# Moving the bias products behind the first x products in the head of a recurrent kernel

## The chip, the cores and the metric

The kernel runs on one core of a Trainium2 chip. The metric is the device time of one execution in microseconds (us), as the median of several runs.

## What is computed

The input x has 16 sequences of 256 steps with 512 features. A GRU cell runs over the steps, and its states feed an expert-choice layer; x is added at the end. What matters here is the cell, in float32:

```
gi = x @ W_ih + b_ih            # 512 -> 3 * 512
gh = h @ W_hh + b_hh
r = sigmoid(i_r + h_r);  z = sigmoid(i_z + h_z)
n = tanh(i_n + r * h_n)
h = (1 - z) * n + z * h         # 256 steps, one after the other
```

The first state is `cond_2048`. The biases are not zero. For r and z both biases can be summed; for n, `b_hh` stands inside the product with r, so it is kept apart. After the recurrence come router logits, a softmax, the choice of the 256 strongest tokens of each of 16 experts, one matrix product with the expert's weights, and a weighted sum.

## The kernel before

**Tiling.** A step has 16 rows. Two steps form a pair, and the products x @ W_ih are made for a pair at once. The 512 output features are split into four groups of 128 partitions in a bank: `quadrant(j)` names 32 partitions of a bank, and four products with `tile_position=(0, 32 * j)` fill the four quadrants side by side. Six PSUM banks hold the sums: `ra` (r gate and input part of n, 256 columns), `hn` (hidden part of n) and `zz` (z gate), each twice, for even and odd pairs. All products add to what the bank holds (`start=False`), so each bank is first given a value.

**The head.** What runs before step 0 is written out by hand, with a fixed order on every engine:

- `begin_sums` (L108) fills a bank with products of zeros. `keep_clock(n)` (L470) repeats this n times on a bank called `idle`, which is otherwise unused; it only keeps TensorE working. It is called with 22 and, behind the x products, with 2.
- `load_rows` (L228) loads W_ih, then W_hh, half on SyncE's queue and half on ScalarE's, in the gate order r, n, z.
- GpSimd's queue loads the biases in three transfers (L288), then x of the first two pairs in eight (L273, `load_pairs(0, 2, ...)`), then clears `c0` and loads the initial state into it in four (L292). A transfer of this queue uses one of eight semaphores in turn, so the ninth waits until the first has landed.
- `biases(i)` (L305) multiplies a column of ones with the bias rows, into the banks of both pairs. VectorE copies the sums of one of them to `bias` and `nb` in SBUF (L481 to L483). They are needed by all later pairs, whose banks ScalarE presets from them (L421 to L433).
- `turn_x` (L255) transposes x of one pair on VectorE; `x_part` (L435, products at L445) adds x @ W_ih of that pair.
- VectorE turns the initial state and copies it to `hs` (L491, L492).

**The steps.** `h_part` (L449, products at L458) adds h @ W_hh in the order r, n, r, n, z. ScalarE makes r (L516), VectorE forms the argument of tanh, ScalarE makes tanh and z, and VectorE the new state, in two halves (L565 to L590). The next step's products need that state. From step 2 on the x products of later pairs, and from the second group of eight steps on the expert's products, fill TensorE's time while it would wait.

Of the kernel before, what the change touches and what calls it, by code (L numbers as in the profile page):

```python
# [13 lines left out]
ALU = mybir.AluOpType  # L14
# [4 lines left out]
def kernel(  # L19
# [34 lines left out]
    nc = tc.nc  # L54
    B, T, D = x.shape
    E = router_w.shape[1]
    P = 128
# [50 lines left out]
    def begin_sums(bank):  # L108

        n = bank.shape[-1]  # L110
        for j in range(KC):
            nc.tensor.matmul(
                bank[QD * j : QD * (j + 1)],
                zero,
                zero[:, 0:E].unsqueeze(1).to_broadcast([P, n // E, E]),
                start=True,
                stop=True,
                tile_position=(0, QD * j),
            )
# [69 lines left out]
    with (  # L189
# [14 lines left out]
        bias = wts.tile([P, 3, P], F32, name="bias")  # L204
        nb = wts.tile([P, P], F32, name="nb")
        rb = wts.tile([P, E], F32, name="rb")

        b_raw = xs[0:2, NG - 4 : NG - 1, :]
        b_n = xs[0:1, NG - 1, :]
# [7 lines left out]
        ra = [bank[:, 0 : 2 * P].rearrange("p (g d) -> p g d", d=P) for bank in banks[0:2]]  # L217
        hn = [bank[:, 0 : 2 * P] for bank in banks[2:4]]
        zz = [bank[:, 0:P] for bank in banks[4:6]]

        def quadrant(j, m=QD):
            return slice(QD * j, QD * j + m)

        def columns(ap, j):

            return ap.rearrange("p (c j i) -> p j c i", j=KC, i=QD)[:, j]

        def load_rows(dst, src, form):  # L228

            rows = src.rearrange(form, c=KC)  # L230
            for h in range(2):
                ks = slice(KC // 2 * h, KC // 2 * (h + 1))
                queues[h].dma_start(out=dst[:, ks, :], in_=rows[:, ks, :])
# [3 lines left out]
        def load_xa(g, xa, j, qs):  # L237

            for o in range(2):
                q = QD * j + B * o  # L240
                qs[o].dma_start(
                    out=xa[q : q + B],
                    in_=x[:, g * TG + o : (g + 1) * TG : 2, j * P : (j + 1) * P],
                )
# [10 lines left out]
        def turn_x(g, xa, pairs=slice(0, TG // 2)):  # L255
            if g not in xT:
                xT[g] = xtp.tile([P, TG // 2, P], F32, name="xt")
            nc.vector.transpose(  # L258
                xT[g][:, pairs, :].rearrange("p q (c r) -> p q c r", c=KC),
                xa[:, pairs, :].rearrange("p q (i c) -> p q c i", c=KC),  # L260
            )
# [5 lines left out]
        with tc.manual_schedule(engines={ET.SP, ET.Activation, ET.Pool}):  # L267
            def load_pairs(p, n, queue):

                for j in range(KC):  # L270
                    for i in range(n):
                        at = 2 * (p + i)
                        queue.dma_start(  # L273
                            out=xa0[quadrant(j), p + i, :],
                            in_=x[:, at : at + 2, j * P : (j + 1) * P].rearrange("b o d -> o b d"),
                        )

            for i, gate in enumerate((0, 2, 1)):
                load_rows(wih[:, :, i, :], w_ih[:, gate * D : (gate + 1) * D], "(p c) n -> p c n")
            for gate in (0, 2, 1):  # L280
                load_rows(whh[:, :, gate, :], w_hh[:, gate * D : (gate + 1) * D], "(c p) n -> p c n")

            for dst, src in (
                (b_raw[0:1], b_ih.rearrange("(o g d) -> o g d", o=1, d=D)),
                (b_raw[1:2], b_hh.rearrange("(o g d) -> o g d", o=1, d=D)),
                (b_n, b_hh[2 * D :].rearrange("(o d) -> o d", o=1)),
            ):
                nc.gpsimd.dma_start(out=dst, in_=src)  # L288
            load_pairs(0, 2, nc.gpsimd)
            nc.gpsimd.memset(c0, 0.0)  # L290
            for j in range(KC):
                nc.gpsimd.dma_start(  # L292
                    out=c0[QD * j : QD * j + B, :].rearrange("b (c i) -> b c i", c=KC), in_=columns(cond, j)
                )
            load_pairs(2, TG // 2 - 2, nc.sync)
            for j in range(KC):
                load_xa(1, xa1, j, (nc.sync, nc.sync))
            nc.sync.dma_start(out=ewr[:, :, E:], in_=expert_w.rearrange("(c p) n -> p c n", c=KC))
            nc.sync.dma_start(out=ewr[:, :, 0:E], in_=router_w.rearrange("(c p) n -> p c n", c=KC))
            nc.sync.dma_start(out=rb, in_=router_b.rearrange("(o e) -> o e", o=1).to_broadcast([P, E]))  # L300
            nc.sync.dma_start(out=eb, in_=expert_b.rearrange("(o d) -> o d", o=1).to_broadcast([P, D]))

        def biases(i):  # L305
            for dst, rows in (
                (ra[i][:, 0, :], b_raw[:, 0, :]),
                (ra[i][:, 1, :], b_raw[0:1, 2, :]),
                (hn[i][:, 0:P], b_n),
                (zz[i], b_raw[:, 1, :]),  # L310
            ):
                for j in range(KC):
                    nc.tensor.matmul(
                        dst[quadrant(j)],
                        ones[0 : rows.shape[0]],
                        columns(rows, j),
                        start=False,
                        stop=True,
                        tile_position=(0, QD * j),
                        skip_group_check=True,  # L320
                    )
# [3 lines left out]
        def of_step(ap, odd):  # L325
            return ap.rearrange("p (c q b) -> p c q b", q=2, b=B)[:, :, odd, :]
# [108 lines left out]
        def x_part(p, k, z):  # L435
            g, pair = divmod(p, TG // 2)
            lhs = xT[g][:, pair, QD * k : QD * (k + 1)]
            for j in range(KC):
                q = quadrant(j)
                dst, rhs = (  # L440
                    (zz[p % 2][q], columns(wih[:, k, 2, :], j))
                    if z
                    else (ra[p % 2][q], columns(wih[:, k, 0:2, :].rearrange("p g d -> p (g d)"), j))
                )
                nc.tensor.matmul(  # L445
                    dst, lhs, rhs, start=False, stop=(k == KC - 1), tile_position=(0, QD * j), skip_group_check=True
                )
# [20 lines left out]
        idle = ps_m.tile([P, D], F32, name="idle", tag="pe")  # L468

        def keep_clock(n):  # L470

            for _ in range(n):
                begin_sums(idle)

        with tc.manual_schedule(engines={ET.PE, ET.DVE}):
            for bank in banks:
                begin_sums(bank)
            keep_clock(22)
            biases(1)
            biases(0)  # L480
            nc.vector.tensor_copy(bias[:, 0:2, :], ra[1])  # L481
            nc.vector.tensor_copy(nb, hn[1][:, 0:P])
            nc.vector.tensor_copy(bias[:, 2, :], zz[1])  # L483
            for pair in range(2):
                turn_x(0, xa0, slice(pair, pair + 1))
            for z in (False, True):
                for pair in range(2):
                    for k in range(KC):
                        x_part(pair, k, z)
            keep_clock(2)  # L490
            nc.vector.transpose(turned, c0)  # L491
            nc.vector.tensor_copy(hs[:, :, 0, :], of_step(turned, 0))  # L492
        make_masks()
# [6 lines left out]
        with tc.manual_schedule(engines={ET.PE, ET.Activation, ET.DVE, ET.Pool, ET.SP}):  # L500
# [4 lines left out]
            for s in range(T):  # L505
                p, odd = divmod(s, 2)
                g, c = divmod(s, TG)
# [105 lines left out]
                elif g + 2 < NG:  # L613
                    if c == KC:
                        xa_next = new_xa()
                    j = c - KC
# [271 lines left out]
```

## Time and profile before

| | |
|---|---|
| median of 3 runs | 1164.77 us (1163.73 to 1165.15) |
| the profiled execution | 1164.63 us, its span 1162.8 us |
| VectorE busy | 703.6 us (61%) |
| ScalarE busy | 336.1 us (29%) |
| GpSimd busy | 100.0 us (9%) |
| granted TensorE clock, mean | 0.996 |

The span reaches from the first to the last instruction of the profiled execution; the rest of its time lies around it. The page divides the span into 40 slices of about 29 us, so the whole head lies in the first. "PEclk" is the clock that TensorE was granted, as a share of the full one. In a timeline each row has the start, the busy time, the engine, the line and the operation, with like instructions merged.

### The profile page before, as it was taken

Reading aid. Unit: us, or ns where it says so; the run is one execution under the profiler, and the core shown is the slowest. Engines: PE = TensorE matmul, PEld = TensorE weight load, DVE = VectorE, ACT = ScalarE, POOL = GpSimd, SP = SyncE. Lnnn points to the kernel's source line nnn. Section 1 sums busy time; section 2 is a strip of 40 time slices with the busy share of each in tenths; the row PEclk is TensorE's granted clock in tenths of the full one; section 3 lists DMA queues with packets and bytes.
Section 4 is the critical chain, followed back from the end, with each engine's and each line's share of the span. In section 5 each row is a group of like instructions: output and inputs, shape, how many; then the busy total and the mean of one; then the engine's idle time right before and its main releaser. Section 6 shows DMA issues by size and latency. Waiting matters only on the chain. (4 is left out here: it accounts for less than half of the span.)

```text
span 1162.8 us, 79365 instructions
## 1 busy us (share of the span) xinstructions
PE 1147.7 (99%) x36025; PEld 1018.4 (88%) x36025; DVE 703.6 (61%) x4078; ACT 336.1 (29%) x1444; POOL 100.0 (9%) x412
## 2 busy tenths in 40 slices
PE   7999999999999999999999999999999999999998
PEld 4899999999999999999999999999999999989742
DVE  1656665666666666666665666666656666665675
ACT  0323223232323232323232322332223222243320
POOL 3000010000000000000000000000000000000000
PEclk8999999999999999999999999999999999999999
DMA  7200000000000000000000000000000000000017
GB/s 231 76 23 20 21 18 22 21 19 19 20 21 20 21 20 21 20 21 21 20 20 21 21 20 18 22 21 20 18 23 20 21 18 23 20 16 14 3 54 240
DMA packets 48854, 38.01 MB, mean 33 GB/s; under 512 B 7968, under 2 KB 40800, under 8 KB 48512
## 3 DMA queue, kind: packets, MB, share of 16 engines
q1 hardware_dynamic: 46272, 29.56, 8.7%
q8 instruction: 283, 4.64, 1.6%
q10 hardware_dynamic: 1632, 3.15, 0.8%
q14 instruction: 59, 0.48, 0.1%
q0 software_dynamic: 608, 0.19, 0.1%
HBM read 24.47 MB, written 8.39 MB: 28 GB/s over the span
## 5 line engine op out<-in xcount | busy, mean ns | idle before, releaser
L458 PE MATMUL gates<-whh,hs 128*16 128x128 f32 x24576 | 723.2, 273 | 3.4 <-DVE hs L590 3.3
L458 PEld LDWEIGHTS gates<-whh,hs 128*16 128x16 f32 x24576 | 675.6, 103 | 9.5 <-DVE hs L590 4.1
L445 PE MATMUL gates<-wih,xt 128*32 128x256 f32 (+1 forms) x8192 | 385.7, 327 | 4.0 <-DVE xt L258 4.0
L445 PEld LDWEIGHTS gates<-wih,xt 128*32 128x32 f32 x8192 | 256.0, 110 | 65.9 <-DVE xt L258 4.3
L516 ACT ACTIVATE r<-gates 128x128 f32<-128x128 f32 x256 | 71.1, 278 | 614.1 <-PE gates L458 614.1
L520 DVE COPY seen<-r 1x1 f32<-1x1 f32 x256 | 36.3, 142 | 330.2 <-ACT r L516 330.2
L569 ACT ACTIVATE t<-t 128x64 f32<-128x64 f32 x512 | 102.9, 248 | 131.6 <-DVE t L567 131.6
L576 DVE STREAM_TRANSPOSE nT<-t 128x64 f32<-128x64 f32 x512 | 100.3, 234 | 49.0 <-ACT t L569 49.0
L579 DVE STREAM_TRANSPOSE zT<-zs 128x64 f32<-128x64 f32 x512 | 121.6, 237 | 0.2 <-issue 0.2
L590 DVE TENSOR_TENSOR hs<-v,nT 128x32 f32<-128x32 f32 x512 | 101.6, 198 | 21.7
L587 DVE TENSOR_TENSOR v<-u,zT 128x32 f32<-128x32 f32 x512 | 104.5, 204 | 8.8
L407 PE MATMUL pe<-ewr,ht 128*32 128x128 f32 x1920 | 97.0, 273 | 0.0
L565 DVE TENSOR_TENSOR t<-r,gates 128x64 f32<-128x64 f32 x512 | 89.7, 217 | 0.0
L567 DVE TENSOR_TENSOR t<-t,gates 128x64 f32<-128x64 f32 x512 | 88.4, 214 | 0.0
L407 PEld LDWEIGHTS pe<-ewr,ht 128*32 128x32 f32 x1920 | 63.6, 110 | 17.4
L582 DVE TENSOR_TENSOR u<-hs,nT 128x32 f32<-128x32 f32 x512 | 78.3, 153 | 0.0
L570 ACT ACTIVATE zs<-gates 128x128 f32<-128x128 f32 x256 | 71.0, 277 | 0.0
L137 PE MATMUL pe<-ewr,ht 128*32 128x256 f32 (+1 forms) x848 | 64.5, 442 | 0.5 <-ACT pe L160 0.5
L617 POOL COPY xa<-hs 32x1 f32<-32x1 f32 x120 | 21.4, 179 | 478.2 <-DVE hs L590 297.4
L333 POOL COPY ht<-hs 128x128 f32<-128x128 f32 (+1 forms) x128 | 46.8, 396 | 160.9 <-DVE hs L590 153.1
L249 POOL COPY xs<-hs 1x1 f32<-1x1 f32 x128 | 22.7, 178 | 338.5 <-DVE hs L590 333.5
L137 PEld LDWEIGHTS pe<-ewr,ht 128*32 128x32 f32 x848 | 25.9, 109 | 27.0 <-issue 16.8
(102 smaller groups left out, 310.1 us busy)
## 6 DMA issues: line engine op xcount, KB each, us to landing
xs<-in_x_dram SPq DMA_DIRECT2D x128, 64.0 KB
xa<-in_x_dram SPq DMA_DIRECT2D x248, 32.0 KB
out_dram<-xs SPq DMA_DIRECT2D x31, 256.0 KB
wih<-in_L_cond_W_ih_dram SPq DMA_DIRECT2D x3, 512.0 KB
wih<-in_L_cond_W_ih_dram ACTq DMA_DIRECT2D x3, 512.0 KB
whh<-in_L_cond_W_hh_dram SPq DMA_DIRECT2D x3, 512.0 KB
whh<-in_L_cond_W_hh_dram ACTq DMA_DIRECT2D x3, 512.0 KB
ewr<-in_L_ffn_expert_w_dram SPq DMA_DIRECT2D x1, 1024.0 KB
```

The lines of the kernel that those rows point to most:

```text
L137: nc.tensor.matmul(pe[q, cols], ht[:, g, k, q], ewr[:, k, E:][:, cols], start=False, stop=(k == KC - 1), tile_position=(0, QD * j), skip_g ...
L407: nc.tensor.matmul(pes[g][quadrant(j), at : at + P], ht[:, g, k, quadrant(j)], ewr[:, k, E + P * quarter : E + P * (quarter + 1)], start=( ...
L445: nc.tensor.matmul(dst, lhs, rhs, start=False, stop=(k == KC - 1), tile_position=(0, QD * j), skip_group_check=True)
L458: nc.tensor.matmul(dst[quadrant(j, m)], lhs, columns(whh[:, k, gate_, :], j), start=False, stop=(k == KC - 1), tile_position=(0, QD * j), ...
L565: nc.vector.tensor_tensor(t[half], r[:, cols], hn[p % 2][:, cols], ALU.mult)
L567: nc.vector.tensor_tensor(t[half], t[half], ra[p % 2][:, 1, cols], ALU.add)
L569: nc.scalar.activation(t[half], t[half], AF.Tanh)
L576: nc.vector.transpose(nT[half], t[half])
L579: nc.vector.transpose(zT[half], zs[:, halves[half][1]])
L582: nc.vector.tensor_tensor(u[half], hs[:, halves[half][2], slot(s), :], of_step(nT[half], odd), ALU.subtract)
L587: nc.vector.tensor_tensor(v[half], u[half], of_step(zT[half], odd), ALU.mult)
L590: nc.vector.tensor_tensor(hs[:, halves[half][2], slot(s + 1), :], v[half], of_step(nT[half], odd), ALU.add)
```

## The change

In GpSimd's queue the eight transfers of x stand first and the three of the biases behind them. The bias products no longer go into the banks of the sums. They are made once, behind the x products and the two rounds of `keep_clock`, into the four 128-column parts of the `idle` bank, which at that point holds zeros. VectorE copies them to `bias` and `nb` and adds them to the sums that the two pairs' banks already hold; ScalarE writes `nb` into the two `hn` banks. Then follow, on VectorE, the turn and the copy of the initial state. 16 bias products take the place of 32. The number of `keep_clock` rounds stays.

```
+            load_pairs(0, 2, nc.gpsimd)
             for dst, src in (
                 (b_raw[0:1], b_ih.rearrange("(o g d) -> o g d", o=1, d=D)),
                 (b_raw[1:2], b_hh.rearrange("(o g d) -> o g d", o=1, d=D)),
                 (b_n, b_hh[2 * D :].rearrange("(o d) -> o d", o=1)),
             ):
                 nc.gpsimd.dma_start(out=dst, in_=src)
-            load_pairs(0, 2, nc.gpsimd)
             nc.gpsimd.memset(c0, 0.0)
...
-        def biases(i):
-            for dst, rows in (
-                (ra[i][:, 0, :], b_raw[:, 0, :]),
-                (ra[i][:, 1, :], b_raw[0:1, 2, :]),
-                (hn[i][:, 0:P], b_n),
-                (zz[i], b_raw[:, 1, :]),
-            ):
+        def biases(bank):
+
+            for i, rows in enumerate((b_raw[:, 0, :], b_raw[0:1, 2, :], b_raw[:, 1, :], b_n)):
                 for j in range(KC):
                     nc.tensor.matmul(
-                        dst[quadrant(j)],
+                        bank[quadrant(j), P * i : P * (i + 1)],
                         ones[0 : rows.shape[0]],
                         columns(rows, j),
...
             keep_clock(22)
-            biases(1)
-            biases(0)
-            nc.vector.tensor_copy(bias[:, 0:2, :], ra[1])
-            nc.vector.tensor_copy(nb, hn[1][:, 0:P])
-            nc.vector.tensor_copy(bias[:, 2, :], zz[1])
             for pair in range(2):
                 turn_x(0, xa0, slice(pair, pair + 1))
             for z in (False, True):
                 for pair in range(2):
                     for k in range(KC):
                         x_part(pair, k, z)
             keep_clock(2)
+            biases(idle)
+
+            nc.vector.tensor_copy(bias, idle[:, 0 : 3 * P].rearrange("p (g d) -> p g d", d=P))
+            nc.vector.tensor_copy(nb, idle[:, 3 * P :])
+            for pair in range(2):
+                nc.scalar.copy(hn[pair][:, 0:P], nb)
+                nc.vector.tensor_tensor(ra[pair], ra[pair], bias[:, 0:2, :], ALU.add)
+                nc.vector.tensor_tensor(zz[pair], zz[pair], bias[:, 2, :], ALU.add)
             nc.vector.transpose(turned, c0)
             nc.vector.tensor_copy(hs[:, :, 0, :], of_step(turned, 0))
```

## The prediction

> **What bounds the kernel now.** I read the page's engine rows, its slices and its costliest group first, then the timeline of the first 27 us engine by engine, then the windows, because the change touches only what runs before the first of 256 recurrence steps.
>
> ```profile
> PE 1147.7 (99%) x36025; PEld 1018.4 (88%) x36025; DVE 703.6 (61%) x4078; ACT 336.1 (29%) x1444; POOL 100.0 (9%) x412
> ...
> PEclk8999999999999999999999999999999999999999
> ...
> L458 PE MATMUL gates<-whh,hs 128*16 128x128 f32 x24576 | 723.2, 273 | 3.4 <-DVE hs L590 3.3
> ```
>
> TensorE is busy all the way and its clock is full everywhere but in the first slice. The recurrence is one serial chain, so a head that hands over 1 us earlier is worth 1 us, and nothing behind it absorbs that. The question is when the first L458 product starts, and at which clock. The timeline of GpSimd, TensorE and VectorE in the head (start, busy time, engine, line; idle time before and what ended it in brackets):
>
> ```profile
> 1.33 0.64 POOL L288 DMA_DIRECT2D xs<-in_L_cond_b_ih_dram  x1 [0.47 <-issue]
> 1.97 0.97 POOL L288 DMA_DIRECT2D xs<-in_L_cond_b_hh_dram  x2
> 2.93 3.02 POOL L273 DMA_DIRECT2D xa<-in_x_dram  x5
> 7.06 0.59 POOL L273 DMA_DIRECT2D xa<-in_x_dram  x1 [1.12 <-DMA xs<-in_L_cond_b_ih_dram]
> 8.65 1.18 POOL L273 DMA_DIRECT2D xa<-in_x_dram  x2 [1.00 <-DMA xs<-in_L_cond_b_hh_dram]
> ```
>
> ```profile
> 3.45 6.51 PE L112 MATMUL idle<-zero 128*32 128x512 bf16 x88
> 9.89 1.96 PE L313 MATMUL gates<-xs,ones 2*32 2x128 f32 x64
> 15.88 7.56 PE L445 MATMUL gates<-wih,xt 128*32 128x256 f32 x128 [4.03 <-DVE xt L258]
> 23.26 0.61 PE L112 MATMUL idle<-zero 128*32 128x512 bf16 x8
> 23.70 2.79 PE L458 MATMUL gates<-whh,hs 128*16 128x128 f32 x96
> ```
>
> ```profile
> 10.60 0.42 DVE L481 COPY bias<-gates 128x256 f32<-128x256 f32 x1 [9.71 <-PE gates L313]
> 10.94 0.28 DVE L482 COPY nb<-gates 128x128 f32<-128x128 f32 x1
> 11.14 0.28 DVE L483 COPY bias<-gates 128x128 f32<-128x128 f32 x1
> 15.42 0.40 DVE L258 STREAM_TRANSPOSE xt<-xa 128x128 f32<-128x128 f32 x1 [4.00 <-DMA xs<-in_cond_dram]
> 16.39 0.41 DVE L258 STREAM_TRANSPOSE xt<-xa 128x128 f32<-128x128 f32 x1 [0.57 <-DMA xa<-in_x_dram]
> ```
>
> GpSimd issues three bias transfers, then x; its last three x transfers wait until the bias transfers have landed. TensorE ends the biases at 11.85 and sits idle for 4.03 us until x is there (the releaser named at 15.42 is the initial state's transfer; by order it is x of pair 0, which shares its semaphore). The windows show the clock (length, PE busy, PEld, DVE, ACT, POOL, then PEclk, DMA share, GB/s):
>
> ```profile
> 6.64:10.06 3.42, 3.42 (x72) 1.52 (x64) 0.00 (x0) 0.00 (x0) 2.00 (x5) 1.00 1.07 327
> 10.06:13.47 3.41, 1.79 (x64) 1.52 (x56) 0.82 (x3) 1.28 (x1) 3.17 (x10) 1.00 1.06 334
> 13.47:16.88 3.41, 1.00 (x12) 0.54 (x16) 0.81 (x2) 0.00 (x0) 0.02 (x1) 0.50 1.06 338
> 16.88:20.30 3.42, 3.42 (x40) 1.55 (x36) 1.46 (x9) 0.00 (x0) 0.30 (x1) 0.50 1.05 386
> 20.30:23.71 3.41, 3.41 (x103) 2.61 (x99) 0.00 (x0) 0.00 (x0) 0.00 (x0) 1.00 0.26 84
> ```
>
> The clock was halved from 13.47 to 20.30, one stretch of 6.83 us, after 1.6 us of idle time in a window that was 52% busy. The halved clock cost the x products half of the 4.42 us from 15.88 to 20.30.
>
> **x earlier.** The eight x transfers now start at 1.33 and follow at 3.02/5 = 0.60 us each, so the seventh (the last of pair 0) starts at 4.96 and the eighth at 5.56. From issue to landing the transfers of this queue took 5.4 us (first bias) to 6.7 us (median of x); the last one of before was issued at 9.24 and turned at 16.39, 7.15 us. I take 7.15, as the DMA engines are as full here (share 1.07), and 5.4 as the other end. Pair 0 is then there at 12.1 (10.4 at the early end) and its products start 0.48 us later as in the rows above (15.40 to 15.88): 12.6 instead of 15.88. The first two gates of wih land by 9.7 in the trace and its third by 14.4, both in time.
>
> **The x products.** Their 7.38 us (15.88 to 23.26) are 4.42 halved and 2.96 full, so 5.17 us at full clock. From 12.6 that gives an end at 17.8 at full clock throughout, 19.5 if the clock is halved from 13.47 to 16.88, and 21.2 if it is halved to 20.30. The window 10.06 to 13.47 would now be busy for 0.9 us instead of 1.79, so a drop is as likely as before; since TensorE now works from 12.6 on, I take the recovery one window earlier than in the trace: 19.5.
>
> **Biases behind it.** The two warming rounds take 0.44 (23.26 to 23.70), and the bias products are half as many, 1.96/2 = 0.98. Their three transfers now wait for the first x transfers to land (about 8 to 9 us) and take 6.5, so they land near 16, under the x products; without that cover every us late is a us lost. The four transfers of the initial state wait for later x transfers as they do now, and stay near 10.3 to 12. Products end at 19.5 + 0.44 + 0.98 = 20.9.
>
> **The new stretch on VectorE.** Before, bias copies and the turning of the initial state lay under other work. Now they stand between the bias products and step 0: a 384-column copy, a 128-column copy, two 256-column sums, two 128-column sums, the turn and the copy of the state. The starts 10.60, 10.94 and 11.14 in the trace give 0.34 us for 256 columns of a copy and 0.20 for 128. So 0.47 + 0.20 + 2 x (0.34 + 0.20) = 1.75 us. The trace has no sum of that size; the sums of the recurrence that read a bank (L565, two of 64 columns in 0.35 us, 0.22 each) start 0.13 apart, which lies on the line of the copies, so I take the copies' price. The upper end is their full duration in place of their spacing, 0.42 and 0.28, 0.3 us more; less than the copies is 0.1 at most. The state's turn and copy took 0.55 us from start to end, and handing over from and to TensorE some 0.27. Together 2.57. Behind these instructions on VectorE wait the state's copy and the small mask operations; the latter have 1.6 us until the first sigmoid ends. Step 0 then starts at 23.5 in place of 23.70: the 3.2 us won in front have gone.
>
> **ScalarE.** In the built order the copies of the n bias into two banks come before the first sigmoid, and there are two table loads where there was one at 10.10, each behind VectorE. A load took 1.28 us. The n bias is there 0.75 us into the stretch, the load ends at 2.05, the copy (0.27) at 2.3, the n products need it at 3.0. The second load ends near 3.8, the first sigmoid is due at 2.57 + 1.56 = 4.1 (23.70 to 25.26 in the trace). I cost both at nothing; uncovered they cost 1.28 each. [...]
>
> **The clock in the recurrence.** TensorE now idles 2.57 us between bias products and step 0, behind 0.98 us of products on two rows only. In the phase of the profile, 20.30 to 23.71 would be busy for about 0.85 us (25%), less than the 52% after which the clock was halved. Then 23.71 to 30.54 (6.83 us, as in the trace) runs at half clock: step 0 has 2.79 - 0.21 = 2.58 us of products left, which take 5.16, and step 1 loses 0.2, together 2.8. The other ends are 1.7 (one window of 3.41, half of it lost) and nothing. I take 2.8, from the only stretch that the trace has. [...]
>
> **Sum** against the profiled execution (1164.63, span 1162.8, 1.8 us around it; the median 1164.77 is 0.14 above): -0.2 + 2.8 = +2.6, so 1167.2. A measurement of this kernel can tell about 0.2% (2.3 us) from no change, so the bounds are 1162.4 and 1167.1.
>
> **Rivals.** Forecast, slower (0.37): clock halved in the x products for one window, and again as the recurrence begins, 1167.2. Slower still (0.10): halved to 20.30, head +1.5, and again, 1164.6 + 1.5 + 2.8 = 1168.9; or x lands no earlier because the DMA engines are full until 16.9, head + 0.98 + 2.57, 1168.2. No measurable change (0.36): only one of the two falls happens; x products at full clock and a fall at step 0, -1.9 + 2.8, 1165.5; a fall in the x products alone, 1164.4 to 1166.1. Faster (0.17): neither gap halves the clock, head 23.70 to 21.8, 1162.7, and with x at the early end 1.7 us less, 1161.0. It decides where a gap of 2.6 us lies across two windows, so that each stays busier than the 52%. For it speaks that both gaps are shorter than the 4.03 of before; against it, that they are two, and that the bias products no longer fill the first one. That the change does not do what it says is the landing case above.
>
> **How the numbers follow.** The faster case lies mostly between 1161.0 and 1163, the slowest at 1168.9, with 0.5 for the sums: 1162.2 to 1169.4 leaves out about 2 in 10. Faster by over 0.2% 0.17, within 0.36, slower 0.47 (0.37 and 0.10).
>
> **What would show it.** First x products near 12.6; VectorE busy for some 2.3 us with TensorE idle before step 0; step 0 at about 23.5; a halved clock beginning within 1 us of it and step 0 lasting about 6.5 us instead of 4.0. A first L458 product before 22 with a full clock behind it would refute the forecast, as would a first sigmoid that waits for a table load.

## The result, and the profile after

The changed kernel takes 1168.7 us (median of 8 runs, 1167.02 to 1171.08); the kernel before took 1164.7 us beside it. The ratio is 1.0038 (95% interval 1.0029 to 1.0047): slower by some 4 us. The forecast was 1167.2 us, within 1162.2 to 1169.4. The profiled execution took 1168.76 us, its span is 1167.0 us, 4.2 us over that of before.

The page still shows TensorE busy nearly throughout, with 99% turned into 98%; the clock's row is the same, since slices of 29 us are too coarse for what follows.

```profile
PE 1147.4 (98%) x35993; PEld 1009.6 (87%) x35993; DVE 704.2 (60%) x4081; ACT 337.8 (29%) x1447; POOL 99.7 (9%) x412
...
PEclk8999999999999999999999999999999999999999
```

The timeline of GpSimd and then of TensorE, as shown of before:

```profile
1.44 4.88 POOL L273 DMA_DIRECT2D xa<-in_x_dram  x8 [0.58 <-issue]
8.43 0.51 POOL L289 DMA_DIRECT2D xs<-in_L_cond_b_ih_dram  x1 [2.10 <-DMA xa<-in_x_dram]
9.15 1.12 POOL L289 DMA_DIRECT2D xs<-in_L_cond_b_hh_dram  x2 [0.21 <-issue]
```

```profile
3.45 5.58 PE L112 MATMUL idle<-zero 128*32 128x512 bf16 x88
13.79 7.64 PE L439 MATMUL gates<-wih,xt 128*32 128x256 f32 x128 [4.76 <-DVE xt L258]
21.25 0.61 PE L112 MATMUL idle<-zero 128*32 128x512 bf16 x8
21.79 1.08 PE L307 MATMUL idle<-xs,ones 2*32 2x128 f32 x32
25.25 4.42 PE L452 MATMUL gates<-whh,hs 128*16 128x128 f32 x96 [2.38 <-DVE hs L489]
30.91 2.83 PE L452 MATMUL gates<-whh,hs 128*32 128x128 f32 x96 [1.24 <-DVE hs L587]
```

The x transfers are issued without a break (4.88 us for eight) and the bias transfers wait for them (2.10 us before the first). The x products start 2.1 us earlier than before (13.79, 15.88), but step 0 starts 1.55 us later (25.25, 23.70), as 2.38 us of idle time stand in front of it, and its products then take 4.42 us in place of 2.79. What VectorE and ScalarE do in the new gap:

```profile
22.94 0.56 DVE L482 COPY bias<-idle 128x384 f32<-128x384 f32 x1 [8.19 <-PE idle L307]
23.41 0.28 DVE L483 COPY nb<-idle 128x128 f32<-128x128 f32 x1
23.61 0.42 DVE L486 TENSOR_TENSOR gates<-gates,bias 128x256 f32<-128x256 f32 x1
23.94 0.29 DVE L487 TENSOR_TENSOR gates<-gates,bias 128x128 f32<-128x128 f32 x1
...
25.00 0.20 DVE L489 COPY hs<-nT 128x64 f32<-128x64 f32 x1
```

```profile
23.78 1.28 ACT L485 ACT_TABLE_LOAD   x1 [23.78 <-DVE nb L483]
25.07 0.47 ACT L485 COPY gates<-nb 128x128 f32<-128x128 f32 x2
25.56 1.28 ACT L513 ACT_TABLE_LOAD   x1
28.08 0.28 ACT L513 ACTIVATE r<-gates 128x128 f32<-128x128 f32 x1 [1.24 <-PE gates L452]
```

VectorE's chain is unbroken from 22.94 to 25.20. ScalarE's second load ends at 26.84, and the first sigmoid still waits 1.24 us for TensorE. The windows are laid along the trace's record of the clock, whose stretches from 4.71 to 28.60 last 6.83, 6.83, 6.83 and 3.41 us. They (length, PE busy, PEld, DVE, ACT, POOL, then PEclk, DMA share, GB/s) show two halved stretches, 11.53 to 18.36 and 25.19 to 28.60:

```profile
8.12:11.53 3.41, 0.91 (x20) 0.24 (x8) 0.00 (x0) 0.00 (x0) 2.45 (x7) 1.00 1.08 295
11.53:14.94 3.41, 1.15 (x12) 0.59 (x16) 0.81 (x2) 0.00 (x0) 2.35 (x8) 0.50 1.06 365
14.94:18.36 3.42, 3.42 (x36) 1.58 (x32) 0.00 (x0) 0.00 (x0) 0.13 (x1) 0.50 1.06 370
18.36:21.77 3.41, 3.41 (x96) 2.45 (x88) 0.00 (x0) 0.00 (x0) 0.00 (x0) 1.00 0.81 291
21.77:25.19 3.42, 1.10 (x36) 0.82 (x32) 2.25 (x11) 1.40 (x2) 0.00 (x0) 1.00 0.09 26
25.19:28.60 3.41, 3.35 (x64) 2.70 (x68) 0.98 (x7) 1.91 (x4) 0.18 (x1) 0.50 0.10 29
```

Both drops here follow a window that was little busy (0.91 and 1.10 of 3.41 us), both recoveries one that was almost full (3.42 and 3.35 us). TensorE's waits hold one thing more that before did not have, the third line:

```profile
PE gates L452 <- DVE hs L587: 3.3, 3, 1.2
PE gates L452 <- DVE hs L489: 2.4, 1, 2.4
PE gates L452 <- issue: 1.0, 1, 1.0
```

At 47.35 us, in step 5, TensorE stops for 1.0 us while nothing that the profile shows holds it.

Adding up from the first sigmoids of both kernels: step 1 is 3.18 us late (1.55 of the start, 1.63 of step 0), step 8 is 4.17 late, the last step 3.83, the span 4.22.

### The profile page after: what moved, and what is told of

Its sections match the earlier page's. It is cut to its first block, busy times and chain, and to the rows that moved or that the text cites. A ratio compares the mean times of both kernels' runs of the same rounds, so it can differ in the third digit from the quotient of the medians.

```text
span 1167.0 us, 79313 instructions
## 1 busy us (share of the span) xinstructions
PE 1147.4 (98%) x35993; PEld 1009.6 (87%) x35993; DVE 704.2 (60%) x4081; ACT 337.8 (29%) x1447; POOL 99.7 (9%) x412
## 5 line engine op out<-in xcount | busy, mean ns | idle before, releaser
L439 PE MATMUL gates<-wih,xt 128*32 128x256 f32 (+1 forms) x8192 | 381.6, 327 | 4.8 <-DVE xt L258 4.8
L439 PEld LDWEIGHTS gates<-wih,xt 128*32 128x32 f32 x8192 | 245.8, 110 | 73.0 <-DVE xt L258 5.3
L401 PE MATMUL pe<-ewr,ht 128*32 128x128 f32 x1920 | 93.8, 273 | 0.0
L401 PEld LDWEIGHTS pe<-ewr,ht 128*32 128x32 f32 x1920 | 59.5, 110 | 19.4
L258 DVE STREAM_TRANSPOSE xt<-xa 128x512 f32<-128x512 f32 (+2 forms) x34 | 37.4, 1101 | 19.7 <-DMA xa<-in_x_dram 12.4
```

Of the source, the lines that this page charges most:

```text
L401: nc.tensor.matmul(pes[g][quadrant(j), at : at + P], ht[:, g, k, quadrant(j)], ewr[:, k, E + P * quarter : E + P * (quarter + 1)], start=( ...
L439: nc.tensor.matmul(dst, lhs, rhs, start=False, stop=(k == KC - 1), tile_position=(0, QD * j), skip_group_check=True)
```

## The experiments

The theory was: x does come earlier; the new stretch on VectorE spends what that wins; the clock is halved behind each of TensorE's two gaps (4.76 and 2.38 us), once under the x products and once under step 0. The rivals were ScalarE's table loads, the landing of data, and no effect of the clock.

**Filling the second gap.**

```
+        idle2 = ps_m.tile([P, D], F32, name="idle2", tag="pe")
...
-        def keep_clock(n):
+        def keep_clock(n, bank=idle):
...
-                begin_sums(idle)
+                begin_sums(bank)
...
             biases(idle)
+            keep_clock(11, idle2)
```

> The changed kernel with 11 more rounds of zero products, into the second bank of the pool, behind the bias products (2.3 us at full clock), so that TensorE works while VectorE copies and sums. Clock theory: no drop as the recurrence begins, step 0 at 25.2 as before this edit and 4.0 us long instead of 5.7, so 1.6 us less than the changed kernel, about 1167.1. Rival (step 0 is long because its sigmoid or its n products wait for the table loads and ScalarE's copies): step 0 stays at 5.7 and the time at 1168.7.

Measured: 1165.96 us, ratio to before 1.0011 (1.0002 to 1.002). TensorE's timeline:

```profile
20.93 2.57 PE L112 MATMUL idle<-zero 128*32 128x512 bf16 x44
23.38 2.81 PE L452 MATMUL gates<-whh,hs 128*16 128x128 f32 x96
27.41 2.83 PE L452 MATMUL gates<-whh,hs 128*32 128x128 f32 x96 [1.22 <-DVE zT L579]
```

Step 0 takes 4.03 us, as before the change, though VectorE's and ScalarE's work is the same, and the granted clock is 1.00 from 22.63 to 26.05, where the changed kernel had 0.50 from 25.19 to 28.60. So its length was the clock's, and the rival falls. The table loads have nothing to spare, though, at full clock in this profile. The first sigmoid follows the second load after 0.02 us:

```profile
23.68 1.28 ACT L516 ACT_TABLE_LOAD   x1
24.98 0.28 ACT L516 ACTIVATE r<-gates 128x128 f32<-128x128 f32 x1
```

It comes 1.60 us after the start of step 0, where the kernel before has 1.56.

The median fell by 2.7 us where 1.6 was expected. In this one profile x products began at 12.57 instead of 13.79 and were at half clock for one window only (12.39 to 15.81), both of which lie ahead of the edit, and no wait of step 5 appeared. The 11 runs fall into two groups: five with a mean granted clock of 0.996 took 1166.9 to 1167.3 us, as expected, and six with 0.997 or 0.998, the profiled one among them, took 1164.3 to 1166.0. From these two groups the author's estimate is that much of the further 1.1 us lies in how long the clock was halved under the x products; what the earlier x and the missing wait add is open.

**Filling the first gap.**

```
-            keep_clock(22)
+            keep_clock(38)
```

> The changed kernel with 38 instead of 22 rounds of zero products ahead of the x products (3.4 us more at full clock), so that TensorE hardly idles until x has landed. Clock theory: the x products take 5.2 us instead of 7.5, step 0 starts near 23.0 instead of 25.25, the second gap still halves the clock; about 2.2 us less, 1166.5. Rival (the x products are held by the landing of x and of the weights, not by the clock): the same 7.5 us and 1168.7.

Measured: 1165.97 us, ratio 1.0008 (0.9999 to 1.0017).

```profile
14.01 5.41 PE L439 MATMUL gates<-wih,xt 128*32 128x256 f32 x128 [0.95 <-DVE xt L258]
19.23 0.62 PE L112 MATMUL idle<-zero 128*32 128x512 bf16 x8
19.78 1.08 PE L307 MATMUL idle<-xs,ones 2*32 2x128 f32 x32
23.24 4.31 PE L452 MATMUL gates<-whh,hs 128*16 128x128 f32 x96 [2.38 <-DVE hs L489]
```

The x products start later than in the changed kernel (14.01) and yet end earlier, after 5.22 us until the next row instead of 7.46. Behind the second gap (2.38 us) the clock is still halved in this profile: it is 0.50 from 22.95 to 26.36, and step 0's products take 4.31. Not so in every run: the fastest (1163.65 us) has a mean granted clock of 1.000, and one halved window of 3.41 us would by estimate (1.7 of 1162 us) take 0.0015 from it. The median fell by 2.7 us where 2.2 was expected. Neither the landing of x nor that of the weights held the x products: they run at a clock of 1.00 (12.71 to 19.53), and that was the difference.

**The new place of the biases alone, with the old queue.**

```
-            load_pairs(0, 2, nc.gpsimd)
             for dst, src in ( ... ):
                 nc.gpsimd.dma_start(out=dst, in_=src)
+            load_pairs(0, 2, nc.gpsimd)
```

> The changed kernel with GpSimd's queue in the order of before (biases first, then x); bias products and VectorE's sums stay behind the x products. This is the second half of the change alone. Theory: x products from 15.9 as before, then 0.44 + 1.08 + 2.4 us, step 0 at about 27.2 instead of 23.7, and a halved clock for one window behind it: 1164.7 + 3.5 + 1.6 = 1169.8; so the queue's order alone is worth some 1 to 2 us of the changed kernel. Rival (the transfers of this queue land when the weights let them, so the order is worth nothing): same as the changed kernel, 1168.7.

Measured: 1171.3 us, ratio 1.0053 (1.004 to 1.0067).

```profile
15.65 7.64 PE L439 MATMUL gates<-wih,xt 128*32 128x256 f32 x128 [5.72 <-DVE xt L258]
23.11 0.61 PE L112 MATMUL idle<-zero 128*32 128x512 bf16 x8
23.65 1.08 PE L307 MATMUL idle<-xs,ones 2*32 2x128 f32 x32
27.12 4.42 PE L452 MATMUL gates<-whh,hs 128*16 128x128 f32 x96 [2.38 <-DVE hs L489]
```

Step 0 starts at 27.12, as worked out (27.2), and its products take the 4.42 us that they took in the changed kernel, where the clock was halved under them. The queue's order is thus worth 2.6 us of medians, more than the 1 to 2 expected (1.87 us in the start of step 0, and 0.5 us by which the wait at step 5 is longer than in the changed kernel's profile). The other half of the change costs 6.6. The time is 1.5 us over the expectation; 1.5 us is also the length of that wait without a named cause.

**Filling the gap of the kernel before.** The prediction's reading of before says that its own idle time of 4.03 us costs clock as well (0.50 from 13.47 to 20.30).

```
             biases(0)
+            keep_clock(18)
```

> The kernel of before with 18 rounds of zero products between the bias products and the x products (3.8 us at full clock), where TensorE idles from 11.85 to 15.88. Clock theory: x products from 15.9 in 5.2 us instead of 7.4, step 0 at 21.5 instead of 23.7, its z products just behind the last gate of whh (about 23.0); 2.2 us less than before, 1162.5. Rival (the weights' landing holds step 0 anyway): no change, 1164.7.

Measured: 1163.54 us, ratio 0.9992 (0.9983 to 1.0001).

```profile
11.30 4.08 PE L112 MATMUL idle<-zero 128*32 128x512 bf16 x72
15.43 5.41 PE L445 MATMUL gates<-wih,xt 128*32 128x256 f32 x128
20.65 0.62 PE L112 MATMUL idle<-zero 128*32 128x512 bf16 x8
21.09 2.80 PE L458 MATMUL gates<-whh,hs 128*16 128x128 f32 x96
```

Step 0 starts at 21.09 in place of 23.70. The x products take 5.22 us to the next row in place of 7.38, and those of step 0 2.80 us, so neither ran at half clock; the mean granted clock is 0.999 in all 11 runs, against 0.994 to 0.997 in those of before and 0.995 or 0.996 in all eight of the changed kernel. But of the 2.6 us only 1.8 are left at step 8: here too TensorE waits 0.8 us without a named cause, at 42.2.

**Both fillings.** Both edits to the changed kernel at once.

> The changed kernel with both fillings: 38 rounds of zero products ahead of x and 11 into a second bank behind the bias products. Clock theory: neither drop; x products 5.2 us from about 13.9, step 0 at 13.9 + 5.2 + 0.44 + 1.1 + 2.4 = 23.0, 4.0 us long; 0.7 us ahead of the kernel before, so about 1164.0 without a wait of TensorE for its code, 1165 with one. Rival (each filling pays by itself, but they overlap, as either moves the clock's windows): no better than one filling alone, 1166.0.

Measured: 1165.47 us, ratio 1.0009 (1.0 to 1.0018). In the profile the x products take 5.23 us to the next row and those of step 0 2.88 us, so neither ran at half clock (the mean is 0.999). Step 0 is at 22.79, and 4.1 us later step 1: 0.85 us ahead of the kernel before at steps 0 to 4. Then TensorE waits 1.57 us without a named cause, and step 8 is 0.54 behind. So the head of this profile does what the theory says, and the time has to be explained from that wait; taken by medians alone the rival could not be told from it. The two slowest of the 11 runs (1167.8 and 1168.55) have a mean clock of 0.997 where the others have 0.999 or 1.000, so by estimate (0.0015 for a halved window of 3.41 us, as above) the clock was halved for one or two windows more in these; no profile of them shows it.

**The table loads.**

```
             nc.gpsimd.memset(c0, 0.0)
+            nc.scalar.activation(nb[0:1, 0:1], ones[0:1, 0:1], AF.Sigmoid)
```

> The changed kernel with a sigmoid of one value at the head of ScalarE's work, so that the one table load lies at about 10 us and both later ones go. Theory (both loads lie beside VectorE's sums and step 0's products): the same as the changed kernel, 1168.7 within 0.5. Rival (a load is waited for by the n products or by the first sigmoid): up to 1.3 us less, 1167.4.

Measured: 1169.72 us (1168.28 to 1172.71), ratio 1.0048 (1.0035 to 1.0062), no less than the changed kernel. ScalarE's timeline:

```profile
10.60 1.28 ACT L291 ACT_TABLE_LOAD   x1 [10.60 <-DMA wih<-in_L_cond_W_ih_dram]
11.89 0.20 ACT L291 ACTIVATE nb<-ones 1x1 f32<-1x1 f32 x1
23.43 0.47 ACT L486 COPY gates<-nb 128x128 f32<-128x128 f32 x2 [11.34 <-DVE nb L484]
27.73 0.28 ACT L514 ACTIVATE r<-gates 128x128 f32<-128x128 f32 x1 [3.83 <-PE gates L453]
```

One load is left, at 10.60, and the first sigmoid still comes 2.84 us after the start of step 0 (24.89), as it did with both loads (2.83). In this kernel, with 4.35 us for the products of step 0, they cost nothing; with the second gap filled and the clock full, they cost 0.04 us at most (1.60 against 1.56 us, as shown above).

**The wait without a cause.** Near step 5 it stands in five of the six profiles of the changed head above (0.5 to 1.7 us; not where the second gap alone was filled) and in the filled kernel of before. In the changed kernel:

```profile
46.72 0.63 PE L452 MATMUL gates<-whh,hs 128*32 128x128 f32 x12
48.33 2.49 PE L452 MATMUL gates<-whh,hs 128*32 128x128 f32 x82 [0.98 <-issue]
```

The page has two queues for instructions:

```profile
q8 instruction: 283, 4.64, 1.7%
q14 instruction: 60, 0.49, 0.1%
```

q8 brings 283 pieces of 16 KB each. That they hold TensorE's code is the author's estimate: no record names the engine, but it has 72 thousand of the 79 thousand recorded instructions, matrix products and weight loads, which would make about 254 to a piece. From step 2 on a step takes 128 products on average, each with a weight load, so by that estimate about one piece in 4 us; in the changed kernel the records have them 3.9 us apart (median). The trace's records of q8 show a common sign. TensorE goes on 2.2 to 2.4 us after a piece begins to arrive (45.91 and 48.33 in the changed kernel, 48.4 and 50.7 with the old queue, 40.68 and 43.0 in the filled kernel of before), and that piece comes late, 6 to 7 us after the one ahead of it. Between the two pieces lies the load of the expert's weights, 1 MB in one transfer (its packets lie from 41.75 to 45.61 in the changed kernel, and for the last 2.6 us of it the DMA engines are full, with a share of 1.01). In all six profiles the late piece begins 0.3 to 0.8 us after the last packet of that load. In the two without a wait (the kernel before, and the changed one with only the second gap filled) the next piece begins 1.4 to 1.6 us after it, and 5.5 to 5.7 us after the piece ahead. So that load was cut up and spread over four steps:

```
-            nc.sync.dma_start(out=ewr[:, :, E:], in_=expert_w.rearrange("(c p) n -> p c n", c=KC))
...
                 if c < KC:
                     load_x(g, c, s)
+                    if g == 0:
+                        nc.sync.dma_start(out=ewr[:, c, E:], in_=expert_w[c * P : (c + 1) * P, :])
```

> The changed kernel with the load of the expert's weights (1 MB in one transfer, near 40 to 48 us) cut into four of 256 KB, issued one for each of steps 0 to 3. Theory (the 1.0 us in which TensorE waits for nothing at 47.4 us is a wait for its code, whose 16 KB transfer stands behind that load): the wait goes, 0.7 to 1.0 us less, 1167.8. Rival (that wait is a chance event or has another cause): a wait of the same size stays near step 4 or 5, 1168.7.

Measured: 1167.08 us, ratio 1.0017 (1.0009 to 1.0026), against 1.0038 (1.0029 to 1.0047) without the edit. TensorE's timeline around step 5:

```profile
46.66 2.83 PE L451 MATMUL gates<-whh,hs 128*32 128x128 f32 x96
49.31 1.49 PE L438 MATMUL gates<-wih,xt 128*32 128x256 f32 x40
```

The wait is gone from this profile. Between 39 and 49 us the pieces of q8 now come at most 4.9 us apart. The median fell by 1.6 us where 0.7 to 1.0 was expected; in this profile the recurrence had a halved clock of 6.83 us (23.30 to 30.12), so the further gain is not one of the head that this run shows. Runs of the same mean granted clock are faster too: 1166.4 to 1168.6 us at 0.995, against 1168.6 to 1171.1 in the changed kernel, and 1165.5 to 1167.1 at 0.996, against 1167.0 to 1168.1.

**Both findings on the kernel of before.** The filled gap and the load cut in four.

> The kernel of before with 18 rounds of zero products behind the biases and the load of the expert's weights cut into four as above. If both theories hold: step 0 at 21.1, no code wait near 42 us, 1162.7, 2.0 us less than before. If the code wait has another cause: as with the filling alone, 1163.5.

Measured: 1163.03 us (1162.11 to 1164.62), ratio 0.9989 (0.998 to 0.9998). The profile has no wait at step 5, and step 255 comes 2.32 us before that of the kernel before. Step 0 starts at 21.67, later than the expected 21.1: TensorE waits 0.42 us without a named cause among the x products (20.14 to 20.55), again behind a late piece of q8 (17.90, 6.7 us after the one ahead). This is the fastest version tried: 1.7 us under the kernel before and 5.7 under the changed one. That the 1 MB load delays the pieces remains the author's estimate and was not shown: two profiles with the cut load have no wait near step 5, but of the eight others two have none either.

## Why the prediction was right, step by step

**x earlier.** Right in kind, too large. I took 7.15 us from issue to landing. The seventh transfer, issued at 5.10, was turned at 13.33, 8.2 us later; the first began at 1.44 and not 1.33. x products started at 13.79, not 12.6: 1.2 us of the miss in the head. The landing differs from one execution to the next, though: in the profile with the second gap filled, which is the same up to there, the turn came at 12.11 and the products at 12.57.

**The x products.** I expected one window of halved clock and an end at 19.5. The clock was halved from 11.53 to 18.36, and they took 7.46 us to the next row instead of 6.9. The forecast kept the windows where they lay in the profile of before (halved 13.47 to 20.30), and they began elsewhere in this execution. With the first gap filled, at a clock of 1.00, the products take 5.22 us, 2.24 less; half of the 4.57 us from 13.79 to 18.36 is 2.28, so the clock was the whole of it.

**Biases and VectorE.** 1.08 us for the bias products (forecast 0.98), 2.38 us of idle time behind them (forecast 2.57). The prices of copies held for sums: 0.42 and 0.29 us, starting 0.33 and 0.20 apart.

So step 0 started at 25.25 where the forecast had 23.5. The head was not a draw (-0.2), it lost 1.55 us.

**ScalarE.** Cost nothing, as forecast, and shown by the run with one early load. The margin was not as forecast: the halved clock put the sigmoid 2.83 us behind the start of step 0, and at full clock, with the second gap filled, the second load ends (24.96) just when the sigmoid is due. Every load shown here took 1.28 us, and where an instruction stood ready behind it, this began within 0.04 us of its end (at 25.07 in the changed kernel, at 24.98 with the second gap filled).

**The clock in the recurrence.** It came, and began within 0.1 us of step 0, but lasted one window of 3.41 us and cost 1.63 us, not 2.8; the prediction had 1.7 for that form and took the other. The run with the load cut in four had the long form, 6.83 us, and there step 0 lasted 6.55 us, 2.5 more than at full clock. In the changed kernel the drop came after a window with 1.10 us of work in it (21.77 to 25.19). Where the windows lie differs: the trace's record of the clock begins at 6.64 in the profile of before and at 4.71 in that of the changed kernel.

**What the sum left out.** The wait at step 5, 1.0 us in the profile, whose cause no run shows (the author's estimate is code that comes late); it leaves 0.65 us at the last step, as the steps behind it are a little shorter than those of before (4.01 and 3.90 us against 4.20 and 4.09). The remaining 0.4 us lie at the very end: the last output transfer is issued 3.83 us later than before, as all ahead of it, and the span ends 4.22 later. Over the other eight profiles that difference lies between -0.1 and 0.8, so the change need not be its cause.

The terms then read: head +1.55 (forecast -0.2), clock +1.63 (+2.8), wait at step 5 +0.65 (none), end +0.4 (none), together 4.2 against 2.6. The forecast's direction rests on two things that the runs show: the work put in front of step 0 (3.46 us from 21.79 to 25.25) and the halved clock under it (1.63 us). What came is none of its cases as a whole: the head is that of "slower still" (halved for two windows, +1.5), the clock of the recurrence the lower end (1.7). That the time lies within the range is partly luck, as the 1.75 us by which the head was priced too low are offset by 1.2 us too many for the clock.

## What to carry to other kernels

Moving work behind a transfer helps only by what it does not then put in front of the next step: here 2.1 us of earlier x bought 3.5 us of bias products and VectorE work on the critical path. A gap of TensorE can have a second price: in the heads profiled here each of the eleven gaps of 2.38 to 5.72 us was followed by products at half clock, or by products as long as at half clock (7.33 to 7.46 us for x, 4.35 and 4.42 us for step 0), and none of the shorter ones (1.28 us and less) was. Rounds of products that nobody reads took that price away: in the kernel before they brought step 0 from 23.70 to 21.09 and the median from 1164.7 to 1163.54 us. Look at the windows on both sides of each gap before moving anything. Where an engine stops and the profile names no cause, compare the records of the instruction queues with those of the large transfers.

## What the runs showed of the hardware that was not expected

One instruction queue, q8, brings 283 pieces of 16 KB. Near step 5 TensorE stopped for 0.5 to 1.7 us in six of the ten profiles, each time behind a piece that came late (6 to 7 us after the one ahead), 0.3 to 0.8 us after the last packet of a 1 MB transfer; in the profiles of both kernels where the transfer was cut in four it did not happen there. That the pieces are TensorE's code, and that it ran out of it, is the author's estimate from these times; no run shows it.

Windows that were not idle were followed by a halved clock. The busiest such window was 60% busy by the records (2.06 of 3.42 us, 19.88 to 23.30, in the run with the load cut in four), but 1.08 us of that were bias products with two rows. In the kernel before, the window ahead of the drop was 52% busy, all of it with bias products (1.79 of 3.41 us, 10.06 to 13.47). In the run with the early load a window was 51% busy with full products, around the wait at step 5, and the full clock stayed:

```profile
45.17:48.58 3.41, 1.74 (x36) 0.88 (x28) 1.56 (x10) 0.68 (x4) 0.18 (x1) 1.00 0.67 191
48.58:52.00 3.42, 3.37 (x116) 3.28 (x120) 1.53 (x11) 0.91 (x4) 0.00 (x0) 1.00 0.03 7
```

So the busy share alone, by which the prediction judged the windows, does not decide; what does was not shown. In the windows shown by these runs the full clock came back after those busy for 2.69 us (13.06 to 16.47) and more and not after one of 2.40 us (23.30 to 26.71); both figures are of the run with the load cut in four.
